# Layer 2 context attention: one place in which an older batch's steps are issued

## The chip, the core and the metric

The kernel runs on one core of a Trainium2 chip. A core has a matrix engine (PE, whose weight loads are shown apart as PEld), a vector engine (DVE), a scalar engine (ACT), a general engine (POOL) and a queue for transfers (SP); each takes its instructions in order, and they wait for each other through semaphores. The metric is device time in microseconds (us) of one execution, the median of several runs. Before the change it is 3500.77 us (three runs, 3495.93 to 3503.63).

## The reference

The reference is a decoder of four layers on x, 8 batches of 256 rows of 256 values; each layer has a self attention, an attention to a context of 77 rows a batch, and a feed-forward part, and each is followed by a layer norm of x plus what the part gave. The change lies in the context attention of layer 2 (`_L2_xattn_ref`) and in the router of the feed-forward part behind it:

```python
q = (x @ q_w.T + q_b).reshape(b, s1, H, hd).transpose(0, 2, 1, 3)
kv = (y @ kv_w.T + kv_b).reshape(b, s2, 2, H, hd).transpose(2, 0, 3, 1, 4)
k, v = (kv[0], kv[1])
q = _layernorm(q, qn_w, qn_b)
k = _layernorm(k, kn_w, kn_b)
q = _apply_rope(q) * scale
attn = jnp.einsum('bhqd,bhkd->bhqk', q, k)
attn = jax.nn.softmax(attn, axis=-1)
o = jnp.einsum('bhqk,bhkd->bhqd', attn, v)
o = o.transpose(0, 2, 1, 3).reshape(b, s1, c)
return o @ out_w.T + out_b
...
# _L2_ffn_ref: 14 routed experts, two of them for each row
gates = jax.nn.softmax(xf @ router_w, axis=-1)
top_v, top_i = jax.lax.top_k(gates, TOP_K)
```

There are 16 heads of 16 values; x has 2048 rows in all, of which each goes to two of the 14 routed experts.

## The kernel before

One program runs the twelve parts one after the other. x stays on chip as 16 tiles of 128 rows, and, transposed, as four tiles `xt`. `l2_xattn` works batch by batch (two tiles of 128 rows). The order of the work is written out by hand, and the build lays it down engine by engine in nearly that order. A pass of the loop for batch b issues:

- `weights(b, q2)`: products of keys and shifted queries (L1837) in two groups, and their exponentials on ACT (L1842);
- `queries(b + 2)`: values and queries (L156 on `cT`, `xt` and `qb`), the query's norm on DVE (L1665 to L1671, L1783);
- `shift(b + 1, ...)`: transposes of the padded queries (L302), the score products (L1814, 32 small matmuls), their maxima on DVE (L1818, eight reductions), then `between`, then the turn of the maxima: eight transposes (L1825) and two additions onto the transposed queries (L1826). With the maximum in an extra row of the query the next pass gets shifted scores;
- as `between`: `weigh(b, e, v)`, products of exponentials and values in two halves (L1856), each copied out (L1862 on ACT, L1858 on DVE);
- `rotated(b + 2, ...)`: the rotary embedding on POOL and DVE (L1794 to L1800).

What ends a batch is put on a list, `todo`, by `self.later`, as a generator. `tick` (line 94) issues the next step of the first entry; a finished entry is taken off and the next one starts in the same tick. `settle_local` (line 110) ticks until no entry that was marked local is left. For each batch the list holds two entries one after the other:

- `heads_out` (line 1391), with `project` and `put_both`: transposes of oT and the division by the row sums (L1398 to L1407); transposes of o (L302); the out projection (L156, `w,oT`) with the residual (L276 on POOL, L281), and the layer norm (L253, L255, POOL L183 and L184, L264); transposes of x into `xt` (L236);
- `Routing.batch` (line 2546): squares of x on ACT (L2554), their root on POOL (`rr`), x scaled (`rx`, L2560), the router products (L156, `rw,xt`), softmax and the two largest (L2578 to L2597), the running counts (L2600, `rbefore`); an empty step; then the rank products (L156, `rsel,upper` and `rbefore,onesb`), ranks and targets (L2609 to L2622), and four scatters of x rows to the experts' slots by POOL (L1041).

In a pass there are ticks in `weights` (two), in `shift` (one before and one behind the score products), in `weigh` (one after each half) and one at the end. Before the change this brings, for the batch before the one that is weighed: o transposes and out projection in `weights`, x transposes and router products in `shift`, the empty step and the rank products in `weigh`; and oT transposes of the batch just weighed at the pass's end. `self.routed` keeps the DVE copy of the second half of weigh behind the running counts.

Behind the stage the feed-forward part starts with `l2_shared` (L1893, L1897, L1907), whose weights `l2s` are loaded on SP and scaled by ACT (L1927), and `tables`, which needs the ranks of all batches.

Of the kernel before, what the change touches and what calls it, by code (L numbers as in the profile page):

```python
# [61 lines left out]
class Build:  # L62
# [1660 lines left out]
    def l2_xattn(self, route):  # L1723
        nc, a = self.nc, self.a
        with ExitStack() as ctx:
# [38 lines left out]
            def queries(b):  # L1764

                v = vps[b % 3]
                ps = self.ps()
                self.mm(ps[:SC, :D], [(self.cT[:, k, b * SC : (b + 1) * SC], W[:, k, 512:768]) for k in range(2)])
                nc.vector.tensor_tensor(
                    v[:SC, :, :16],  # L1770
                    ps[:SC, :D].rearrange("p (h d) -> p h d", h=H),
                    self.row("l2x_kvb")[:SC, D:].rearrange("p (h d) -> p h d", h=H),
                    ALU.add,
                )
                ps = self.ps()
                for t in range(2):
                    self.mm(
                        ps[:, t * D : (t + 1) * D],
                        [(self.xt(k, 2 * b + t), W[:, k, :256]) for k in range(2)] + [(one[:1], qb[:1])],
                    )  # L1780
                r = self.deviations(w2, ps.rearrange("p (n d) -> p n d", d=16), 32)
                q = self.t(w2, [P, 2, H, 16], "q")
                nc.vector.tensor_tensor(  # L1783
                    q.rearrange("p t h d -> p (t h) d"), ps.rearrange("p (n d) -> p n d", d=16),
                    r.unsqueeze(2).to_broadcast([P, 32, 16]), ALU.mult,
                )
                return q, v

            def rotated(b, q, v):
                qp = qpad[b % 3][:, :, :, :16]  # L1790
                over = lambda t: t.unsqueeze(2).to_broadcast([P, 2, H] + list(t.shape[2:]))
                u1, u2 = (self.t(w2, [P, 512], n).rearrange("p (t h d) -> p t h d", t=2, h=H) for n in ("sq", "u2"))
                for u in range(2):
                    nc.gpsimd.tensor_tensor(  # L1794
                        u2[:, :, :, u::2], q[:, :, :, 1 - u :: 2], over(other[:, :, :, u]), ALU.mult
                    )
                flat = lambda t: t.rearrange("p t d u -> p t (d u)")
                nc.vector.tensor_tensor(u1, q, over(flat(own)), ALU.mult)
                nc.vector.tensor_tensor(u1, u1, over(flat(more)), ALU.add)
                nc.gpsimd.tensor_tensor(qp, u1, u2, ALU.add)  # L1800
                return qpad[b % 3], v

            def shift(b, qp, between=None):

                qT = self.t(w2, [P, 4, S], "qT")
                for t in range(2):
                    self.transpose_to(qT[:, :, t * P : (t + 1) * P], qp[:, t].rearrange("p h d -> p (h d)"), 4)
                self.tick()
                tiles = [slice(t * P, (t + 1) * P) for t in range(2)]
                for t, c in enumerate(tiles):  # L1810
                    ps = [self.ps()[:, : 4 * SC].rearrange("p (g s) -> p g s", g=4) for j in range(4)]
                    for g in range(4):
                        for j, r in enumerate(rows):
                            nc.tensor.matmul(  # L1814
                                ps[j][:, g, :], qT[r, g, c], kT[r, g, b * SC : (b + 1) * SC], start=True, stop=True
                            )
                    for j in range(4):
                        nc.vector.tensor_reduce(mxps[t][:, :, j, 16], ps[j], AX.X, ALU.max, negate=True)  # L1818
                self.tick()
                if between is not None:  # L1820
                    between()
                for t, c in enumerate(tiles):
                    pt = self.ps().rearrange("p (g s) -> p g s", g=4)
                    for g in range(4):
                        nc.tensor.transpose(pt[:, g, :], mxps[t][:, g].rearrange("p j d -> p (j d)"), self.ident)  # L1825
                    nc.vector.tensor_tensor(qT[:, :, c], pt, qT[:, :, c], ALU.add)  # L1826
                return qT

            def weights(b, q2):

                e = []
                for gp in range(2):
                    ps = [self.ps()[:SC].rearrange("p (g s) -> p g s", g=2) for j in range(4)]
                    for i in range(2):
                        for j, r in enumerate(rows):
                            g = 2 * gp + i
                            nc.tensor.matmul(  # L1837
                                ps[j][:, i, :], kT[r, g, b * SC : (b + 1) * SC], q2[r, g, :], start=True, stop=True
                            )
                    o = self.t(w2, [SC, 4, 2, S], "e", bufs=2)  # L1840
                    for j in range(4):
                        nc.scalar.activation(o[:, j], ps[j], AF.Exp, scale=0.25)  # L1842
                    e.append(o)
                    self.tick()
                return e

            def weigh(b, e, v):

                o = self.t(w2, [P, 4, S], "oT")
                routed, self.routed = self.routed, None  # L1850
                for gp in range(2):
                    ps = self.ps().rearrange("p (g s) -> p g s", g=2)
                    for i in range(2):
                        for j, r in enumerate(rows):
                            h = 4 * (2 * gp + i) + j
                            nc.tensor.matmul(ps[r, i, :], v[:SC, h, :], e[gp][:, j, i, :], start=True, stop=True)  # L1856
                    if gp:
                        ins = nc.vector.tensor_copy(o[:, 2 * gp : 2 * gp + 2, :], ps)  # L1858
                        if routed is not None:
                            self.after(ins.ins, [routed.ins])  # L1860
                    else:
                        nc.scalar.copy(o[:, 2 * gp : 2 * gp + 2, :], ps)  # L1862
                    self.tick()
                self.settle_local()
                self.later(self.heads_out(b, o, W[:, :, 768:1024], "l2x_ob", w2, route=route))

            self.routed = None
            ahead = [rotated(0, *queries(0))]
            begun = queries(1)
            q2 = shift(0, ahead[0][0])  # L1870
            ahead.append(rotated(1, *begun))
            for b in range(NB):
                e, v = weights(b, q2), ahead[0][1]
                ahead.pop(0)
                if b + 2 < NB:
                    begun = queries(b + 2)
                if b + 1 < NB:
                    q2 = shift(b + 1, ahead[0][0], lambda: weigh(b, e, v))
                else:
                    weigh(b, e, v)  # L1880
                if b + 2 < NB:
                    ahead.append(rotated(b + 2, *begun))
                self.tick()
# [1079 lines left out]
```

## Time and profile before

| | |
|---|---|
| median of the runs | 3500.77 us |
| the profiled execution's own time | 3466.69 us |
| its span, first to last instruction | 3465.0 us |
| mean granted PE clock | 0.913 |
| the stage: first score products to first L1893 | 2436.1 to 2652.8 us |
| starts of the eight score products | 2436.1, 2453.8, 2475.7, 2503.5, 2531.1, 2558.5, 2585.8, 2612.2 us |

The profile is of one execution. Lines of it name start and length in us, the engine, the line of the kernel, the operation, and tiles as out<-in; in square brackets stands how long the engine was idle before it, and what released it. In a table of stretches each engine has its busy time and the number of its instructions. The granted clock is the share of full speed that PE was allowed. A busy PE is not PE at its peak, since matmuls overlap.

### The profile page before, as it was taken

Reading aid. Unit: us, or ns where it says so; the run is one execution under the profiler, and the core shown is the slowest. Engines: PE = TensorE matmul, PEld = TensorE weight load, DVE = VectorE, ACT = ScalarE, POOL = GpSimd, SP = SyncE. Lnnn points to the kernel's source line nnn. Section 1 sums busy time; section 2 is a strip of 40 time slices with the busy share of each in tenths; the row PEclk is TensorE's granted clock in tenths of the full one; section 3 lists DMA queues with packets and bytes.
Section 4 is the critical chain, followed back from the end, with each engine's and each line's share of the span. In section 5 each row is a group of like instructions: output and inputs, shape, how many; then the busy total and the mean of one; then the engine's idle time right before and its main releaser. Section 6 shows DMA issues by size and latency. Waiting matters only on the chain. (4 is left out here: it accounts for less than half of the span.)

```text
span 3465.0 us, 49405 instructions
## 1 busy us (share of the span) xinstructions
PE 3068.0 (89%) x19135; PEld 2169.0 (63%) x19146; DVE 1819.0 (52%) x4852; ACT 1055.4 (30%) x2386; POOL 911.1 (26%) x1370
## 2 busy tenths in 40 slices
PE   4777679989998998998999999898888998888789
PEld 3444357768886666665566776565555886676556
DVE  7887556641005656785111221576675344777652
ACT  4666422222222233332111111343222112344211
POOL 2222323343313211232000000322343454322241
PEclk6777779989999999999999999999777999988899
DMA  9900110025532000001010333100002562000000
GB/s 334 333 1 6 34 42 16 16 94 185 187 128 89 17 28 14 17 17 59 14 37 25 113 131 118 37 20 8 7 19 84 200 210 77 25 1 7 13 6 19
DMA packets 132672, 241.58 MB, mean 70 GB/s; under 512 B 14600, under 2 KB 103952, under 8 KB 124752
## 3 DMA queue, kind: packets, MB, share of 16 engines
q1 hardware_dynamic: 108176, 138.34, 11.8%
q0 software_dynamic: 23104, 98.95, 8.3%
q8 instruction: 155, 2.54, 0.3%
q10 hardware_dynamic: 1152, 1.05, 0.1%
q14 instruction: 85, 0.70, 0.1%
HBM read 158.61 MB, written 79.69 MB: 69 GB/s over the span
## 5 line engine op out<-in xcount | busy, mean ns | idle before, releaser
L156 PE MATMUL ps<-xt,w 128*128 128x256 f32 (+1 forms) x1408 | 444.6, 465 | 8.3 <-issue 8.3
L156 PE MATMUL ps<-w,hT 128*128 128x256 f32 (+1 forms) x1792 | 397.4, 380 | 0.0
L156 PEld LDWEIGHTS ps<-w,hT 128*128 128x128 f32 (+1 forms) x1792 | 330.5, 187 | 55.9 <-issue 6.0
L156 PE MATMUL ps<-gT,w 128*128 128x256 f32 (+1 forms) x1472 | 356.9, 401 | 5.7 <-ACT gT L144 3.0
L156 PEld LDWEIGHTS ps<-xt,w 128*128 128x128 f32 x1408 | 263.8, 194 | 150.5 <-issue 129.8
L156 PEld LDWEIGHTS ps<-gT,w 128*128 128x128 f32 x1472 | 276.8, 191 | 76.1 <-ACT gT L144 3.9
L156 PE MATMUL ps<-w,oT 128*128 128x256 f32 x768 | 184.1, 394 | 12.3 <-DVE oT L1423 11.2
L156 PEld LDWEIGHTS ps<-w,oT 128*128 128x128 f32 x768 | 147.7, 196 | 48.6 <-issue 12.6
L1147 ACT ACTIVATE hT<-ps,more 128x256 f32<-128x256 f32 x152 | 71.9, 473 | 199.1 <-PE ps L156 199.1
L236 PE MATMUL ps<-ident,x 128*128 128x128 f32 x320 | 64.8, 314 | 74.2 <-DVE x L264 57.3
L276 POOL TENSOR_TENSOR xb<-x,rows 128x256 f32<-128x256 f32 x96 | 74.0, 778 | 212.7 <-DVE res L281 205.5
L264 DVE TENSOR_SCALAR x<-res,mv,rs 128x256 f32<-128x256 f32 x128 | 58.8, 459 | 123.0 <-POOL rs L184 123.0
L1158 DVE COPY y<-ps 128x512 f32<-128x512 f32 x41 | 28.3, 690 | 174.6 <-PE ps L156 174.6
L1224 DVE TENSOR_TENSOR hT<-hT,ps 128x512 f32<-128x512 f32 x56 | 38.5, 687 | 150.6 <-PE ps L156 150.6
L686 ACT ACTIVATE e<-ps,nm 128x128 bf16<-128x128 f32 (+1 forms) x256 | 103.7, 459 | 40.1 <-DVE nm L681 24.1
L1220 ACT ACTIVATE hT<-ps 128x512 f32<-128x512 f32 x56 | 33.4, 597 | 238.5 <-PE ps L156 238.5
L1717 POOL TENSOR_TENSOR kpad<-kpad,rows 128x256 f32<-128x256 f32 (+1 forms) x10 | 7.3, 729 | 363.5 <-DVE hu L1666 276.2
L236 PEld LDWEIGHTS ps<-ident,x 128*128 128x128 f32 x320 | 39.5, 155 | 98.9 <-DVE x L264 44.9
L903 POOL TENSOR_TENSOR P<-P,z 128x1232 f32<-128x1232 f32 (+1 forms) x32 | 55.2, 1734 | 167.3 <-DVE z L902 167.3
L970 PE MATMUL ps<-PT,V 77*64 77x256 f32 x512 | 90.8, 413 | 6.9 <-ACT PT L144 4.4
L1581 ACT ACTIVATE f<-ps,neg 128x512 f32<-128x512 f32 x128 | 77.3, 688 | 57.7 <-PE ps L1578 57.7
L1582 DVE SCALAR_TENSOR_TENSOR f<-ps,f 128x512 f32<-128x512 f32 x128 | 79.1, 682 | 26.1 <-ACT f L1581 26.1
(665 smaller groups left out, 6344.7 us busy)
## 6 DMA issues: line engine op xcount, KB each, us to landing
l2x<-zero SPq DMA_DIRECT2D x28, 1024.0 KB, 11.4
l0x<-zero SPq DMA_DIRECT2D x16, 1024.0 KB, 11.4
w<-in_L_ffn_rg SPq DMA_DIRECT2D x8, 1024.0 KB, 7.1
w<-in_L_ffn_ru SPq DMA_DIRECT2D x8, 1024.0 KB, 5.0
w<-in_L_ffn_rd SPq DMA_DIRECT2D x8, 1024.0 KB, 5.4
l2e<-y SPq DMA_DIRECT2D x22, 256.0 KB, 2.3
rows<-in_rows SPq DMA_DIRECT2D x9, 544.0 KB, 3.7
l0e<-y SPq DMA_DIRECT2D x19, 256.0 KB, 2.7
```

Of the source, the lines that this page charges most:

```text
L156: self.nc.tensor.matmul(out, lhsT, rhs, start=(i == 0), stop=(i == last))
L236: self.nc.tensor.transpose(ps[:, k * P : (k + 1) * P], x[:, k * P : (k + 1) * P], self.ident)
L264: nc.vector.tensor_scalar(t, r, mv[:, 0:1], rs, ALU.subtract, ALU.mult)
L276: self.nc.gpsimd.tensor_tensor(t, self.X[i], row, ALU.add)
L686: nc.scalar.activation(e[:, : (t + 1) * P], ps[j][:, i, :], AF.Exp, bias=nm[:, t, h : h + 1], accum_out=z[:, t, h : h + 1],)
L903: eng.tensor_tensor(pr, pr, z.unsqueeze(2).to_broadcast([P, n, SC]), ALU.mult)
L970: nc.tensor.matmul(po[64 * m : 64 * m + 64, :S], V[:, h * 64 : (h + 1) * 64], ahead[n % 2][:, m, :], start=True, stop=True,)
L1147: nc.scalar.activation(hT[:, f + m, :], ps[:, m * 256 : (m + 1) * 256], func, bias=more[:, f + m : f + m + 1])
L1220: nc.scalar.activation(hT[:, f, :], ps, func, **({"bias": bias(f)} if bias else {}))
L1224: nc.vector.tensor_tensor(hT[:, f, :], hT[:, f, :], ps, ALU.mult)
L1581: nc.scalar.activation(f[:, j], ps[j], AF.Exp, bias=neg1)
L1582: self.mark = nc.vector.scalar_tensor_tensor(f[:, j], ps[j], 1.0, f[:, j], ALU.max, ALU.min)
```

## The change

The second half of `weigh` is no longer followed by a tick, and what followed the two halves, `settle_local` and the putting of `heads_out` on the list, becomes a function `end` of its own. It is called when `shift` is done, that is behind the turn of the maxima. In the last pass, without a shift, it is called right after `weigh`.

```diff
                     else:
                         nc.scalar.copy(o[:, 2 * gp : 2 * gp + 2, :], ps)
-                    self.tick()
+                    if not gp:
+                        self.tick()
+                return b, o
+
+            def end(b, o):
                 self.settle_local()
                 self.later(self.heads_out(b, o, W[:, :, 768:1024], "l2x_ob", w2, route=route))
...
+                out = []
                 if b + 1 < NB:
-                    q2 = shift(b + 1, ahead[0][0], lambda: weigh(b, e, v))
+                    q2 = shift(b + 1, ahead[0][0], lambda: out.append(weigh(b, e, v)))
                 else:
-                    weigh(b, e, v)
+                    out.append(weigh(b, e, v))
+                end(*out[0])
                 if b + 2 < NB:
                     ahead.append(rotated(b + 2, *begun))
                 self.tick()
```

With one tick fewer in a pass, and nothing else asking for a step, the remaining ticks find earlier steps of the list than before. No instruction is added or taken away.

## The prediction

> **What bounds the kernel now.** I read the page first, then the one stage that the change touches. The page:
>
> ```profile
> span 3465.0 us, 49405 instructions
> PE 3068.0 (89%) x19135; PEld 2169.0 (63%) x19146; DVE 1819.0 (52%) x4852; ACT 1055.4 (30%) x2386; POOL 911.1 (26%) x1370
> PEclk6777779989999999999999999999777999988899
> ```
>
> PE bounds the kernel as a whole. The context attention of layer 2 lies at 2436 to 2653 us: its three slices of about 87 us are the dip to 7 in the PEclk row. Next, the stretches of the stage. A batch is counted from one start of the score products (L1814) to the next; the columns are the stretch, its length, busy time of PE, PEld, DVE, ACT and POOL, granted clock, DMA share, GB/s:
>
> ```profile
> 2503.50:2531.13 27.63, 23.88 (x196) 17.18 (x196) 18.96 (x70) 7.20 (x19) 11.17 (x16) 0.75 0.06 21
> 2558.50:2585.84 27.34, 22.30 (x196) 15.76 (x196) 19.46 (x70) 7.20 (x19) 11.17 (x16) 0.81 0.06 21
> 2612.23:2652.87 40.64, 30.60 (x245) 21.96 (x245) 22.93 (x95) 11.48 (x28) 13.99 (x23) 0.67 0.34 118
> ...
> 2492.45:2506.10 13.65, 12.45 (x110) 8.65 (x106) 6.69 (x21) 6.50 (x16) 7.07 (x12) 1.00 0.11 38
> 2506.10:2519.75 13.65, 11.10 (x88) 8.38 (x87) 12.16 (x50) 0.71 (x2) 3.59 (x4) 0.50 0.01 2
> ```
>
> A batch takes 27.3 to 27.9 us, no engine fills it, and the clock is two-valued inside it: half speed from the score products to the turn, full speed for the rest. So this stage is a chain between PE and DVE. The waits of PE over five such batches, and the steps of one of them:
>
> ```profile
> PE ps L156 <- DVE rsel L2597: 11.0, 5, 2.7
> PE ps L1814 <- DVE mxp L1818: 5.7, 5, 1.2
> ```
>
> ```profile
> 2503.50 1.13 PE L1814 MATMUL ps<-l2kT,qT 32*128 32x77 f32 x32 [0.16 <-ACT qT L144]
> ...
> 2509.38 1.89 PE L156 MATMUL ps<-rw,xt 128*128 128x14 f32 x8
> ...
> 2511.19 3.64 PE L1856 MATMUL ps<-e,vp 77*32 77x256 f32 x32
> ...
> 2516.29 0.20 PE L156 MATMUL ps<-rsel,upper 128*128 128x14 bf16 x1 [1.46 <-DVE rsel L2597]
> ...
> 2516.71 1.74 PE L1825 MATMUL ps<-ident,mxp 128*128 128x128 f32 x7
> ...
> 2518.24 1.78 PE L1398 MATMUL ps<-ident,oT 128*128 128x128 f32 x8
> ...
> 2523.48 1.99 PE L156 MATMUL ps<-w,oT 128*128 128x256 f32 x8
> ...
> 2525.86 0.17 DVE L255 BATCH_NORM_AGGREGATE mv<-st 128x2 f32<-128x6 f32 x1
> ...
> 2527.71 0.41 DVE L264 TENSOR_SCALAR x<-res,mv,rs 128x256 f32<-128x256 f32 x1 [0.92 <-POOL rs L184]
> ...
> 2529.16 0.41 DVE L264 TENSOR_SCALAR x<-res,mv,rs 128x256 f32<-128x256 f32 x1 [0.95 <-POOL rs L184]
> ```
>
> PE waits 11.0/5 = 2.2 us a batch in front of the rank products (L156, rsel) for the router's selection, with the turn (L1825) behind them though its maxima are ready. That wait is what the change goes at. But the older batch's norm (res, aggregate, x, then rx at 2531.22) runs beside the query products of 2525.10 to 2529.44, where PE has work that does not need it.
>
> **The change, part by part.** *Rank products behind the turn.* The turn's transposes (1.74 us) and its two adds on DVE no longer stand behind the rank products. In a batch where nothing else moves this saves at most the wait and the turn that stood behind it: 1.46 + 1.74 = 3.2 us.
>
> *One step fewer per batch.* The steps of the older batch come off one list, one per tick, and the rank step has an empty step ahead of it. With the second tick of `weigh` gone, the built order lets the rank products and then w,oT fall back in the third batch of the stage (they start at 2436.09, 2453.80, 2475.65 and so on) and the rest in the fourth; from the fifth (now 2531.13), every step of the older batch stands one place later. PE then has: score products, out projection (w,oT), half of weigh, x transposes, other half, turn, router products, half of the weights' products (L1837), rank products, other half, transposes of oT, queries. DVE has the norm, rx, the oT copy and the two adds of the turn behind the eight maxima, then the router's softmax.
>
> I walk one such batch at full clock, from the first score product at 0. The maxima end at 2511.41 - 2503.50 = 7.9 now; without the xt copy (0.33) and two rx (0.62) ahead of them, with an oT copy (0.33), 7.3. Two res and two stats (0.34, 0.34, 0.40, 0.40 to the next) and the aggregate: 9.0. From the aggregate to the first x is 1.85 us (2525.86 to 2527.71), to the second 1.45 more, to rx 2.06 more: 10.8, 12.3, 14.3. PE has done w,oT and half of weigh by about 8.3 and waits about 3 us for x. Two rx 0.62, oT copy 0.60, two adds 1.29: the turn is complete at 16.8, against 2519.17 - 2503.50 = 15.7 now. The router's softmax follows on DVE: 2.7 us without other work between (2638.75 to 2641.43 in the last batch), so rsel at 19.5 and the rank products done at 20.0, against 13.2 now. Half of L1837 1.0 (2519.95 to 2520.98), oT transposes 0.9 (as the eight of qpad, 2529.44 to 2530.37), queries 4.3 (2525.10 to 2529.44), transposes of qpad and o 1.3: next score products at 27.5. So at full clock the batch is no shorter than the 27.4 of now: **0**. The wait for rsel is back (about 2 us: 1.0 us of products stands before it where 3.64 of weigh stood), and a wait for x is new.
>
> *The clock on that path.* Now the half-speed stretch ends 3.46 us after the rank products (2516.29 to 2519.75), in the unbroken PE work that follows them. In the new order unbroken work begins only at 20.0, so the half speed should last till 23.5. At half speed the other half of weigh, the turn and the router products (1.82, 1.74 and 1.89 by their rows) put the softmax back from 16.8 to about 18.5: +1.7. The half of L1837 and the oT transposes take 1.8 each in place of 1.0 and 0.9 (half of weigh takes 1.07 at 2631.42 at full speed, 1.82 above; the oT transposes' 1.78 is above): +1.7. Sum **+3.4** a batch, two full batches: **+6.8**. Bounds 0 (full clock) and +5.1 (two query products of 0.86 at half speed too).
>
> *Third and fourth batch*: the wait ahead of the turn is saved, but the softmax now shares DVE with the turn and half speed lasts past the rank products. Bounds -3.2 and 0 each; I take **0**, by the clock row.
>
> *The seventh batch* (2585.84 to 2612.23, 26.39 us, no queries): 27.5 - 4.3 + 1.7 = 24.9, so -1.5; its softmax may come later by the same 1.7: between -1.5 and +0.2. I take **-0.5**.
>
> *The end.* The before already shows the new order once: in the last batch w,oT starts at 2629.49, weigh's halves (1.07 and 1.54) lie between, and router products come only at 2636.82. In the changed kernel batch 6 is a step further back, weigh runs ahead of its w,oT and covers nothing: 2.6 (1.07 + 1.54) to 3.64 (a whole weigh at half speed); **+3.0**.
>
> *Queues.* SP: the five loads of l2s and l3wd pass ahead of the reload of rows; its first reader is at 2890, so 0, covered by 230 us of L2 FFN; were it not, one landing of 3.7 us. POOL: the same adds, rsqrts and four scatters a batch, the rope product (L1800, 1.27) now between rs and rr; POOL is busy 11.2 of 27.6, the scatters' reader comes after the stage. ACT: two l2s scalings (1.33) now stand between the squares of batch 6: 0 to 1.3, **+0.5**.
>
> The sum: 0 + 6.8 - 0.5 + 3.0 + 0.5 = **+9.8 us**. The profiled execution took 3466.69 (span 3465.0 and 1.69 around it), so 3476.5 on its terms; the median of the runs is 3500.77, 34 us (1.0%) above it, and I add the difference to that: **3510.6 us**.
>
> A rule weighed. "TensorE: Matmul & The Clock Gate", section "Why this matters for your kernels" of the Trainium skill, says that a kernel keeps full speed without PE gaps of over about 3 us. Here the clock fell to 0.50 at 2506.10 with no PE wait above 1.2 us in front of the score products, and no longer one within 10 us before, so the trace does not agree; by the page the new wait of 3 us would just pass, the clock would not fall, and the sum would be that of the first rival.
>
> **The rivals.** *The clock recovers early (other side).* If weigh and turn, now adjacent, bring full speed before the rank products, both middle batches keep 3.2 and the full ones cost 0: -6.4 + 0 - 1.5 + 3.0 + 0.5 = -4.4, 3496.4 us. It decides if PE's stretch between score products and rank products is granted 1.00. For it: full speed came back 3.5 us into unbroken work. Against it: the new wait for x breaks that work.
>
> *The wait is simply gone (faster).* If POOL's rs comes some 3 us sooner and x is there when half of weigh ends, only the saved waits count: -11.0, 3489.8 us. Against it: 1.85 and 1.45 us from aggregate to x in every batch.
>
> *Half speed reaches the queries:* 2 x 5.1 + 3.64 + 1.3 = +15.1, 3515.9 us.
>
> **How the numbers follow.** A change below 0.2% (7 us) can hardly be told from none. Chances: the forecast 0.55 (own range 3505 to 3515; 0.07 of it below +7), half speed further 0.12, clock recovers 0.18, wait gone 0.15. Slower: 0.48 + 0.12 = 0.60; same: 0.07 + 0.18 = 0.25; faster: 0.15. The range leaves out most of the fastest case and the top of the slowest, and adds the runs' own 4 us: 3493 to 3520.
>
> **What would show it.** Right: in the after, batches five and six at 30 to 31 us; a PE wait at L236 for x of 2 to 4 us; L156 still waiting for rsel about 2 us; half clock past the rank products; about 3 us more from the last score products to the first router work of the FFN (L1893 here). Wrong if those batches are at or under 27 us, or the clock in the stage rises above 0.8 while L236 does not wait.

## The result, and the profile after

The changed kernel takes 3515.22 us (median of six runs, 3512.55 to 3521.26) beside 3498.35 us for the kernel before (six runs, 3490.62 to 3503.63): a ratio of 1.0049, 95% interval 1.0033 to 1.0065. That is 16.9 us slower, where +9.8 was forecast.

The page of the profile of the changed kernel (its lines for the span, the busy time, and the granted clock in 40 slices):

```profile
span 3511.4 us, 49401 instructions
PE 3087.6 (88%) x19135; PEld 2169.0 (62%) x19146; DVE 1821.1 (52%) x4852; ACT 1057.4 (30%) x2386; POOL 912.0 (26%) x1370
PEclk6777789989999999999999999998776999988899
```

No work was added, yet PE is busy 19.6 us longer than in the profile before, and the dip to 7 in the clock row reaches 6. The page alone decides nothing, since a second profile of the kernel before (the last experiment) has PE busy for 3092.6 us; the stage has to be read by itself. From the first score product to the first product of the feed-forward part (L1893 before, L1899 now), it went from 216.78 to 241.18 us: +24.4. The stage before, then after (columns as in the prediction: stretch, length, busy time and records of PE, PEld, DVE, ACT, POOL, granted clock, DMA share, GB/s):

```profile
2436.09:2652.87 216.78, 176.68 (x1521) 125.56 (x1521) 142.19 (x503) 59.40 (x144) 79.13 (x110) 0.76 0.10 35
```

```profile
2457.17:2698.35 241.18, 188.64 (x1521) 127.93 (x1521) 142.83 (x503) 61.94 (x144) 79.41 (x110) 0.71 0.09 32
```

Behind it, 812.11 and 813.04 us remain. The two profiled executions also differ by 21 us in unchanged code ahead of the stage. That is scatter between executions: the second profile of the kernel before starts its stage at 2459.67 us, where the first had 2436.09.

The stretches of the stage in the changed kernel: batches five, six and seven, and the end:

```profile
2555.07:2587.92 32.85, 26.13 (x197) 17.54 (x197) 19.62 (x72) 7.73 (x19) 11.42 (x15) 0.69 0.05 17
2587.92:2619.70 31.78, 23.70 (x198) 16.26 (x197) 19.72 (x72) 7.79 (x19) 11.38 (x15) 0.73 0.05 18
2619.70:2648.44 28.74, 22.04 (x181) 15.36 (x180) 19.25 (x70) 7.31 (x18) 11.38 (x15) 0.64 0.04 15
2648.44:2698.35 49.91, 36.43 (x257) 24.21 (x257) 26.39 (x105) 13.02 (x34) 16.94 (x29) 0.63 0.29 99
```

A fifth batch that took 27.37 us with 22.28 us of PE now takes 32.85 with 26.13, of the same 197 records, at a clock of 0.69 in place of 0.81. The end holds 12 records more than before (257, it was 245). Over the whole stage PE is busy 188.64 us (176.68 before) and idle 52.54 (40.10): the 24.4 us are 12.0 of the same products done more slowly and 12.4 of waits.

The waits of PE over the third to seventh batch (line, what it waited for, us in total, times, longest), in the kernel before those for the norm's x alone, then in the changed kernel:

```profile
PE ps L236 <- DVE mv L255: 1.9, 1, 1.9
PE ps L236 <- DVE x L264: 1.0, 1, 1.0
```

```profile
PE ps L236 <- DVE mv L255: 8.8, 3, 4.0
PE ps L1814 <- DVE mxp L1818: 8.3, 5, 3.6
PE ps L156 <- DVE rsel L2603: 7.5, 5, 3.5
PE ps L236 <- DVE x L264: 6.7, 3, 2.3
```

The wait for the router's selection fell from 11.0 to 7.5 us, and 15.5 us of waiting for the norm's x (L236) are there where 2.9 were. The steps of the sixth batch, in order of time (start, length, engine, line, operation, tiles; idle time and its releaser in brackets):

```profile
2591.65 1.99 PE L156 MATMUL ps<-w,oT 128*128 128x256 f32 x8
...
2593.57 1.07 PE L1856 MATMUL ps<-e,vp 77*32 77x256 f32 x16
...
2598.65 0.66 PE L236 MATMUL ps<-ident,x 128*128 128x128 f32 x2 [4.01 <-DVE mv L255]
...
2601.37 0.66 PE L236 MATMUL ps<-ident,x 128*128 128x128 f32 x2 [2.07 <-DVE x L264]
...
2601.96 1.94 PE L1856 MATMUL ps<-e,vp 77*32 77x256 f32 x16
...
2603.83 1.97 PE L1825 MATMUL ps<-ident,mxp 128*128 128x128 f32 x8
...
2610.09 0.19 PE L156 MATMUL ps<-rsel,upper 128*128 128x14 bf16 x1 [0.84 <-DVE rsel L2603]
...
2612.32 1.94 PE L1398 MATMUL ps<-ident,oT 128*128 128x128 f32 x8
```

It is the order that the prediction walked. The out projection stands behind the score products, half of `weigh` (1.07 us, full clock) covers little of the norm, PE waits 4.0 and 2.1 us for x, and the other half takes 1.94 us: the clock has fallen to 0.50 meanwhile (from 2597.0 to 2614.1 by the clock's record, 17.1 us; 10.2 in the fifth and sixth batch before).

Batch by batch, against the kernel before:

| | before | after | difference | forecast |
|---|---|---|---|---|
| batches 1 and 2 | 39.6 | 38.1 | -1.5 | 0 |
| batch 3 | 27.85 | 30.97 | +3.1 | 0 |
| batch 4 | 27.64 | 28.86 | +1.2 | 0 |
| batch 5 | 27.37 | 32.85 | +5.5 | +3.4 |
| batch 6 | 27.35 | 31.78 | +4.4 | +3.4 |
| batch 7 | 26.39 | 28.75 | +2.4 | -0.5 |
| the end | 40.64 | 49.91 | +9.3 | +3.5 |

The -1.5 of the first two batches is not the change's: the second profile of the kernel before takes 38.05 us for them.

### The profile page after: what moved, and what is told of

The parts are those of the page before. It is cut to its first block, busy times and chain, and to the rows that moved or that the text cites. A ratio compares the mean times of both kernels' runs of the same rounds, so it can differ in the third digit from the quotient of the medians.

```text
span 3511.4 us, 49401 instructions
## 1 busy us (share of the span) xinstructions
PE 3087.6 (88%) x19135; PEld 2169.0 (62%) x19146; DVE 1821.1 (52%) x4852; ACT 1057.4 (30%) x2386; POOL 912.0 (26%) x1370
## 3 DMA queue, kind: packets, MB, share of 16 engines
q1 hardware_dynamic: 108176, 138.34, 11.8%
q10 hardware_dynamic: 1152, 1.05, 0.1%
## 5 line engine op out<-in xcount | busy, mean ns | idle before, releaser
L236 PE MATMUL ps<-ident,x 128*128 128x128 f32 x320 | 66.3, 317 | 95.0 <-DVE x L264 70.8
L264 DVE TENSOR_SCALAR x<-res,mv,rs 128x256 f32<-128x256 f32 x128 | 61.5, 480 | 123.6 <-POOL rs L184 123.6
L1158 DVE COPY y<-ps 128x512 f32<-128x512 f32 x41 | 28.3, 691 | 171.5 <-PE ps L156 165.6
L236 PEld LDWEIGHTS ps<-ident,x 128*128 128x128 f32 x320 | 39.2, 156 | 123.9 <-issue 61.4
L1582 DVE SCALAR_TENSOR_TENSOR f<-ps,f 128x512 f32<-128x512 f32 x128 | 79.1, 682 | 26.2 <-ACT f L1581 26.2
```

The source lines that it names most:

```text
L236: self.nc.tensor.transpose(ps[:, k * P : (k + 1) * P], x[:, k * P : (k + 1) * P], self.ident)
L264: nc.vector.tensor_scalar(t, r, mv[:, 0:1], rs, ALU.subtract, ALU.mult)
L1582: self.mark = nc.vector.scalar_tensor_tensor(f[:, j], ps[j], 1.0, f[:, j], ALU.max, ALU.min)
```

## The experiments

The change does two things at once: it puts the rank products behind the turn, and it takes a step out of each pass, which puts the older batch's steps a place later. Theory: the lost place costs, through waits for x and a longer half-speed stretch, and the exchange is free or a gain. Rival: the exchange itself costs.

The time that stands beside a measured one is that of the kernel before in the same comparison; it differs between comparisons (3469.87 to 3498.26 us). Stages, batches and waits are those of one profiled execution each.

**The exchange alone.** One more step inside `end`, so that all other steps stay at their old places:

```diff
             def end(b, o):
+                self.tick()
                 self.settle_local()
```

> The changed kernel, with one more step of the list issued inside `end`, ahead of settle_local. Each pass so has as many steps as before the change, and PE's order is the old one but for one exchange: the rank products come behind the turn. Theory (the lost place costs, the exchange does not): w,oT stays in front of the queries, the stage takes 205 to 218 us (216.8 before, 241.2 with the whole change), PE does not wait for x at L236 over 0.5 us, and the time is 0 to 10 us under the kernel before. Rival (the exchange itself costs, because the turn's two adds on DVE and the rank work get in each other's way): the stage takes 225 us or more and the time is 8 us or more above the kernel before.

Measured: 3498.51 us beside 3469.87, ratio 1.0080 (1.0066 to 1.0095), and a stage of 239.43 us. The rival holds: batches three to seven take 33.48, 32.15, 30.80, 30.79 and 31.37 us with every step but one at its old place, and PE waits 17.6 us in them for rsel, where it waited 11.0. One such batch:

```profile
2589.50 0.17 DVE L2586 TENSOR_TENSOR rs<-ps,rm 128x28 f32<-128x28 f32 x1
...
2591.21 1.97 PE L1825 MATMUL ps<-ident,mxp 128*128 128x128 f32 x8
2592.43 0.69 DVE L1826 TENSOR_TENSOR qT<-ps,qT 128x512 f32<-128x512 f32 x1 [2.76 <-PE ps L1825]
...
2593.04 0.17 DVE L2588 TENSOR_REDUCE rm<-rs 128x2 f32<-128x28 f32 x1
...
2596.69 0.17 PE L156 MATMUL ps<-rsel,upper 128*128 128x14 bf16 x1 [3.51 <-DVE rsel L2604]
```

DVE's queue has changed too. The turn's first add (L1826) now stands between the softmax's subtraction (L2586) and its sum (L2588). The exponentials were ready at 2590.4, but DVE stands 2.76 us at the add, which waits for PE's turn, which waits behind `weigh`. So rsel is done 15.5 us after the first score product (2581.17), where in the fifth batch before it was 12.5 (2543.67 - 2531.13), and the rank products wait 3.5 us for it with nothing left to cover it.

**The lost place alone.** The kernel before with the step behind the second half of `weigh` taken away, and `settle_local` and `later` at their old place ahead of the turn:

```diff
-                    self.tick()
+                    if not gp:
+                        self.tick()
```

> The kernel before with only the step behind the second half of weigh taken away; settle_local and the putting on the list stay inside weigh, ahead of the turn. In this order the router products come ahead of the turn and the rank products behind it. Theory (the lost place costs): batches five and six take 30 to 33 us, PE waits 4 to 6 us a batch for x at L236, the stage takes 232 to 245 us, the time is 10 to 20 us above the kernel before. Rival (the exchange costs, not the place): batches at 27 to 28 us and the time within 5 us of the kernel before.

Measured: 3487.68 beside 3469.87 us, ratio 1.0059 (1.0039 to 1.0079), stage 237.69 us; batches five and six 33.16 and 33.63, with 14.8 + 11.8 us of waits for x in the stage. As the theory expected, with batches even longer than its 30 to 33 us. The lost place is not wholly alone here: the rank products come behind the turn in this order too, and the third batch (30.99 us, with a wait of 3.5 us for rsel) is that of the changed kernel. In batches five to seven PE does not wait for rsel at all, so their length is put down to the lost place. Either half of the change makes the stage some 20 us longer by itself, and the two do not add up: once the router's products come behind the turn, the turn's adds have nothing left to push back (the same dependency in the changed kernel, below).

**DVE's order restored.** The kernel of the first experiment, with the turn's adds held behind the router's running counts, as they stood before:

```diff
+                self.chosen = routed
...
-                    nc.vector.tensor_tensor(qT[:, :, c], pt, qT[:, :, c], ALU.add)
+                    ins = nc.vector.tensor_tensor(qT[:, :, c], pt, qT[:, :, c], ALU.add)
+                    if between is not None and self.chosen is not None:
+                        self.after(ins.ins, [self.chosen.ins])
```

> The kernel with the rank products behind the turn and all steps at their old places (e1_order), with the two adds of the turn on DVE held behind the router's running counts by a dependency, as DVE's order was before the change. Theory (the exchange costs because the turn's adds slip ahead of the softmax's sum on DVE, which then stands 2.8 us waiting for PE's turn): rsel comes 12.5 to 13 us after the first score product in place of 15.3, PE waits about 1 us or less for it, a steady batch takes 26 to 27.5 us in place of 30.8 to 33.5, the stage 205 to 217, and the time is 0 to 10 us under the kernel before. Rival (the half clock or the place of the rank products costs, whatever DVE does): batches at 29 us or more, time 10 us or more above the kernel before.

Measured: 3491.01 us beside 3497.78, ratio 0.9976 (0.9963 to 0.9989): faster than the kernel before. The stage takes 214.42 us. Its steps in one batch, and the stretch they lie in:

```profile
2561.40 3.64 PE L1859 MATMUL ps<-e,vp 77*32 77x256 f32 x32
...
2564.97 1.97 PE L1825 MATMUL ps<-ident,mxp 128*128 128x128 f32 x8
...
2566.26 0.19 DVE L2607 TENSOR_TENSOR rsel<-rhot 128x28 bf16<-128x28 f32 x1
...
2566.74 0.22 PE L156 MATMUL ps<-rsel,upper 128*128 128x14 bf16 x1
...
2567.94 1.28 DVE L1826 TENSOR_TENSOR qT<-ps,qT 128x512 f32<-128x512 f32 x2
```

```profile
2553.71:2580.96 27.25, 23.28 (x196) 16.25 (x197) 18.90 (x70) 7.20 (x19) 11.11 (x16) 0.81 0.06 20
```

rsel is done 12.7 us after the first score product (2553.71), PE works through the turn in the time in which it used to wait, and the wait for rsel is gone. One dependency on DVE turns +28 us into -7, each against the kernel before in its own comparison, and a stage of 239.43 us into 214.42: the cause of the exchange's cost is settled. Only with that order is the exchange a gain, and a small one: 0.1 to 0.5 us a batch against the first trace of the kernel before, 0.8 to 1.2 against the second, where the prediction had it save up to 3.2.

**The same dependency in the changed kernel** (the diff is the one above, on the changed kernel):

> The changed kernel with the dependency of e6_dve: the two adds of the turn stand behind the running counts of the router, where those were issued before. In batches three and four the router is still ahead of the turn, from the fifth on its products come behind it. Theory (two causes, each with its batches): batches three and four go from 30.97 and 28.86 us to 27 to 28, the fifth and later stay within 0.7 us of what they were, the stage goes from 241.2 to 234 to 238 us, the time stays 10 us or more above the kernel before. Rival (one cause, DVE's order): all batches come back to 27 to 28 and the stage to under 225 us.

Measured: 3516.61 beside 3498.26 us, ratio 1.0056 (1.0037 to 1.0075), stage 237.78. The third batch falls to 27.56 us, the fourth, against the theory, stays at 28.85, and the later ones don't move (32.87, 31.81, 28.76, end 49.86). So DVE's order cost 3.4 us in the changed kernel, in the third batch alone. There the changed kernel's own trace had it: DVE is idle for 3.78 us at the first add, with the softmax's sum behind it:

```profile
2503.78 0.17 DVE L2585 TENSOR_TENSOR rs<-ps,rm 128x28 f32<-128x28 f32 x1
...
2507.74 0.69 DVE L1826 TENSOR_TENSOR qT<-ps,qT 128x512 f32<-128x512 f32 x1 [3.78 <-PE ps L1825]
2508.35 0.17 DVE L2587 TENSOR_REDUCE rm<-rs 128x2 f32<-128x28 f32 x1
```

**What the wait for x is worth.** The norm's scale without POOL's reciprocal root, in this stage alone; once on the changed kernel, once on the kernel before:

```diff
-        nc.vector.tensor_scalar(t, r, mv[:, 0:1], rs, ALU.subtract, ALU.mult)
+        nc.vector.tensor_scalar(t, r, mv[:, 0:1], mv[:, 1:2] if self.short else rs, ALU.subtract, ALU.mult)
```

> The changed kernel; in the context attention of layer 2 alone, x is scaled by the variance itself instead of by POOL's reciprocal root, which is still worked out but which nothing waits for (the norm of that part is so left out; later values differ, so the stage alone is read). Theory (in the changed order the batch is set by the older batch's norm, because PE waits 4 to 6 us for x): the waits at L236 fall to 1 to 3 us a batch, the fifth and sixth batch from 32.9 and 31.8 us to 28 to 30, and the stage from 241 to 222 to 232 us. Rival (the router's softmax and the half clock set it, the wait for x only moves): the batches stay at 31 us or more and the stage at 236 or more.

> The kernel before with the same edit as e5_norsq: in the context attention of layer 2 x is scaled by the variance, and nothing waits for POOL's reciprocal root. Theory (the norm is covered by the queries in the old order and by nothing in the new one): the steady batches stay within 0.5 us of 27.4 us, only the last stretch gets shorter, and the stage falls by 3 to 10 us, from 216.8 to 207 to 214, where the changed kernel's fell by 22.2. Rival (the norm weighs the same in both orders, and e5 only took it out): the stage falls by 15 us or more.

Measured: the changed kernel's stage falls from 241.18 to 219.02 us (batches five and six 30.08 and 28.73, with waits of 3.1 us each ahead of the x transposes in place of 4.7 and 6.1), that of the kernel before to 202.24. The stages of the two, the changed kernel first:

```profile
2454.70:2673.72 219.02, 180.24 (x1522) 123.25 (x1521) 139.31 (x503) 61.88 (x144) 78.55 (x108) 0.74 0.10 35
```

```profile
2457.35:2659.59 202.24, 168.35 (x1522) 118.57 (x1521) 141.34 (x503) 61.47 (x144) 78.06 (x107) 0.78 0.11 37
```

By the first alone the theory would have looked proved: 22.2 us of the 24.4 come back. The second takes most of that away. The same edit is worth 14.5 us in the old order too, more than the 3 to 10 expected and just under the rival's 15, half of it in the end (40.64 to 33.33 us). Against the second trace of the kernel before, which is of the same comparison and whose stage is 218.62 us, it is worth 16.4 us: the rival's figure. What the change costs without the root is 219.02 - 202.24 = 16.8 us, so the wait for the root accounts for 24.4 - 16.8 = 7.6 us of the difference by the first trace of the kernel before, and for 22.6 - 16.8 = 5.8 by the second. And of the 16.8, 11.9 (180.24 - 168.35) is PE's busy time: as much as with the root (12.0 by the first trace, 10.3 by the second). The slower products are a second part of the cost, which does not go away with the wait.

**The clock.** Ten products that nobody reads, ahead of the x transposes, where PE waits:

```diff
                     if not gp:
+                        pf = self.ps()
+                        for n in range(10):
+                            nc.tensor.matmul(pf[:, :D], self.ident, W[:, 0, :D], start=True, stop=True)
                         self.tick()
```

> The changed kernel, with ten products of 128x128 by 128x256 of which nobody reads the result, in each pass between the first half of weigh and the x transposes, where PE waits 4 to 6 us for x. They take 2.5 us at full clock and 5 at half, 8 passes. Theory (half of the loss is the clock: PE busy grew by 12.0 of the stage's 24.4 us with the same products): the granted clock of the stage rises from 0.71 to 0.78 or more, batches five and six go from 32.9 and 31.8 to 28 to 30 us, and the time falls to within 8 us of the kernel before in spite of the added products. Rival (DVE and POOL set the batch, whatever the clock): batches five and six stay at 31 to 33 us or grow, and the time is 14 us or more above the kernel before.

Measured: 3492.02 beside 3469.87 us, ratio 1.0069 (1.0053 to 1.0085); stage 236.91 us at a clock of 0.84. The sixth batch:

```profile
2575.42:2606.06 30.64, 26.71 (x218) 19.57 (x217) 19.37 (x72) 7.67 (x19) 11.41 (x15) 0.83 0.05 18
```

The ten take 4.58 us at full clock, not 2.5: the trace has two records for such a product, and the estimate counted records. Without them PE is busy 26.71 - 4.58 = 22.1 us in the batch, where the changed kernel needs 23.70 and the kernel before 22.30. Half speed takes 10.2 us of this batch, by the clock's record, where it took 17.1. So the changed kernel's longer PE time is the clock, as the theory has it, and with the clock back the batch is 1.1 us shorter in spite of 4.58 us of added work. The size was missed: the batch was to take 28 to 30 us and the time to come within 8 us of the kernel before, and it is 22 us above, as the rival had it. The added products cost more than the clock gives.

**The same in the kernel before.** Six such products where it waits for rsel:

```diff
                             self.after(ins.ins, [routed.ins])
+                        pf = self.ps()
+                        for n in range(6):
+                            nc.tensor.matmul(pf[:, :D], self.ident, W[:, 0, :D], start=True, stop=True)
```

> The kernel before, with six products of 128x128 by 128x256 that nobody reads between the second half of weigh and the rank products, where PE waits 1.5 to 2.7 us for rsel. By the ten of e4_filler (4.58 us at full clock) they take 2.7 us at full clock and 5.4 at half. Theory (the half clock lasts because PE's columns are few there): the half-speed stretch ends 3 to 7 us sooner in a batch, turn and oT transposes fall from 1.7 to 1.0 us each, the granted clock of the stage goes from 0.76 to 0.85 or more; with up to 2.7 us of added products sticking out the batch stays within 1.5 us of 27.4 and the time within 10 us of the kernel before. Rival (the clock doesn't follow the products): the clock stays below 0.8, batches take 29 to 31 us and the time is 10 us or more above.

Measured: 3517.21 beside 3497.78 us, ratio 1.0058 (1.0039 to 1.0077); stage 240.52 us, clock 0.79, batches 30.6 to 30.8 us. PE in one of them:

```profile
2569.77 4.64 PE L1863 MATMUL ps<-w,ident 128*128 128x256 f32 x12
...
2574.50 0.96 PE L1825 MATMUL ps<-ident,mxp 128*128 128x128 f32 x7
2575.29 1.12 PE L1398 MATMUL ps<-ident,oT 128*128 128x128 f32 x8
```

The turn's seven transposes take 0.96 us (1.74 before) and the oT transposes 1.12 (1.72), as the theory has it. But this does not show that the products brought the clock back. The half-speed stretch of this batch lasts 10.2 us, as in the fifth batch before, and ends 14.6 us after the first score product in place of 16.0, where 3 to 7 us sooner was expected; the turn now starts at 15.5, where it started at 12.7. So it is at full clock mostly because it comes later. The six take 4.64 us, most of it at half clock, in place of a wait of 2.7 at most, and clock, batches and time are all the rival's.

**The end.** The changed kernel with the missing step put back in the last pass:

```diff
-                    if not gp:
+                    if not gp or b + 1 == NB:
                         self.tick()
```

> The changed kernel, with the step behind the second half of weigh kept in the last pass alone. Theory (the +9.3 us from the last score products to the first work of the feed-forward part come of weigh being issued ahead of batch 6's steps): that stretch goes from 49.9 to 42 to 46 us, and the time is 3 to 8 us under the changed kernel, so 8 to 14 above the kernel before. Rival (batch 6 is late by then whatever the last pass issues): 48 to 51 us and the time of the changed kernel, 14 to 20 above.

Measured: 3493.74 beside 3469.87 us, ratio 1.0082 (1.0062 to 1.0102); the end 49.86 us, the length that the rival expected. But it settles nothing: in the built order PE's steps of the last pass stay where they were, so the step put back moved nothing that PE does there. What the end holds is read from the counts above instead: 12 records more, which are the eight of an out projection and the four of a batch's x transposes. No run tests it.

**Both kernels again.**

> The changed kernel as it is, on the chip of this comparison. Theory (the whole difference lies in the stage, which was 24.4 us longer in the two traces): ratio 1.006 to 1.008, stage 239 to 243 us, batches as in the first trace. Rival (the difference depends on more than the stage): ratio 1.0033 to 1.0055 with a stage of 241 again, so that some 7 us come back elsewhere.

> The kernel before as it is, for a trace on the chip of this comparison. Theory (the stage has the same length on every chip and in every run, and the scatter of the medians lies outside it): stage 216.5 to 217.0 us, batches as in the first trace, whatever the total. Rival (the stage scatters with the total): another stage by over 1 us.

Measured: the changed kernel again at ratio 1.0054 (1.0035 to 1.0072; medians 3520.80 and 3497.78), with a stage of 241.18 us as in its first trace; the kernel before with a stage of 218.62 where the first trace had 216.78:

```profile
2459.67:2678.29 218.62, 178.31 (x1521) 126.37 (x1521) 139.74 (x503) 60.97 (x144) 78.73 (x109) 0.76 0.10 35
```

The first expectation can't be decided by the ratio, whose interval holds both. (The ratios are taken as recorded; the quotient of the two medians here is 1.0066.) The second fell: the old order has at least two courses, one with batches of 27.4 us and one with 28.2 (the clock in the fifth is 0.81 or 0.76). So the change costs 22.6 to 24.4 us in the stage. Against this second trace the rows of the table are 0.0, +2.8, +0.7, +4.4, +3.6, +1.4 and +9.6 us.

The medians differ by 16.9 us in the first comparison and by 23.0 here. Why the first is less than the stage's difference is left open; its interval reaches 22.7 us. The changed kernel's two profiled executions differ by 14.6 us (3511.39 and 3525.98 us of span with the same stage), of which 13.7 lie behind the stage (813.04 and 826.78 us).

## Why the prediction was right, and where it was wrong

The sign, the wait that goes, the wait for x that takes its place and the longer half-speed stretch are all there. The sum of +9.8 is short of the stage's +22.6 to +24.4. That the measured 3515.22 us lies in the stated 3493 to 3520 is in part luck: the stage's difference, put on the 3498.35 us of the kernel before, gives 3521 to 3523. The signs named for being right came, but larger than stated: batches five and six at 32.9 and 31.8 us for 30 to 31, waits for x of 4.7 and 6.1 us for 2 to 4, an end longer by 9.3 us for about 3.

- *Batches three and four, 0 each.* This step failed. It said that the wait ahead of the turn is saved and its bounds were -3.2 and 0: a loss was left out without a reason. The third batch lost 3.1 us, and the dependency of one experiment gave 3.4 back. The prediction walked PE's new order and took DVE's order as given by data; the trace shows DVE standing 3.78 us at the turn's add with the softmax behind it. The same cause makes the exchange alone cost 3.4 to 5.6 us a batch, where the prediction's first part had it save up to 3.2. The fourth batch's +1.2 has another cause. In its trace PE stands 3.64 us ahead of the second group of score products, where it stood 1.09, for maxima of which the first starts 4.7 us after the first score product in place of 3.4; the older batch's norm (L281 to L264) stands ahead of it on DVE. This is read from the trace, and no run tests it.
- *Batches five and six, +3.4 each.* Right mechanism, undersized: +5.5 and +4.4. The walk had first x at 10.8, second x at 12.3, the turn complete at 18.5 in its half-clock case, which makes rsel 21.2; the sixth batch has 10.2, 12.0, 18.6 and 22.1. The fifth has nearly the same four. So both run as walked up to the turn. PE's waits for x, 4.7 and 6.1 us where about 3 was walked, are longer because the second x took 1.34 us in both, where the row of before had 0.41, and in the sixth because PE has half of `weigh` done at 6.7 us, where the walk had 8.3. The term that was too small lies behind the turn: the softmax starts only when the router products, 1.73 us at half clock, are done, at 19.4, where the walk let it start with the turn's end at 18.5. That 0.9 is most of what the sixth batch is over the forecast. The fifth is 1.1 us longer still: half speed lasts to 28.3 us of the batch (26.2 in the sixth; 23.5 was walked) and so into the first of the query products (1.91 us for `w,cT`, 1.05 at full clock), which is what the third rival described.
- *The wait for rsel.* About 2 us were walked with half of L1837 at 1.0; at half clock that half takes 2.00 and the wait is 0.84. The two misses cancel.
- *Batch seven, -0.5.* Measured +2.4 (+1.4 by the second trace): the walk took its clock for nearly that of before; it was 0.64, where it was 0.80.
- *The end, +3.0 and +0.5.* Measured +9.3, the largest miss. The step costed only the cover that `weigh` no longer gives. It left out that with the steps a place later, one more out projection and a batch's x transposes (12 records) come behind the last score products, with their own waits, and that all of it runs at a mean clock of 0.63: +5.8 us busy and +3.4 idle. This is read from the trace; the run made to test it moved nothing.
- *The rivals.* The clock did not recover early (0.69 and 0.73 in the full batches). "The wait is simply gone" was given a condition, that x comes some 3 us sooner. The runs without the root come nearer to it without meeting it, since PE still waits 3.1 us in each of batches five and six, and the change still costs 16.8 us there. That speaks against this rival and does not refute it. "Half speed reaches the queries" was seen in the fifth batch; its +15.1 is nearest to the measured 16.9, but by a sum that also lacks the third batch and most of the end.
- *The rule weighed.* "TensorE: Matmul & The Clock Gate" of the Trainium skill, section "Why this matters for your kernels", asks for no PE gap over about 3 us. In the changed kernel's fifth batch the longest gaps are 2.41 and 2.32 us and half speed lasts 17.1 us; in the fastest variant no gap of a middle batch is over 1.2 us and half speed still takes 10.2 of 27.25. The measurement disagrees with the rule in both. In the changed kernel's sixth batch the gap is 4.01 us and the clock does fall within it, so that batch does not speak against the rule.

Put together, not as exact shares, since the parts overlap: of the 22.6 to 24.4 us some 5.8 to 7.6 are PE waiting for the norm's root, 3.4 are DVE's order in the third batch, and 10.3 to 12.0 are the same products at a lower clock (of which 1.9 go with DVE's order).

## What to carry to other kernels

When a step is moved on one engine, look at what the build does on the others: a short add slipped ahead of a softmax on DVE cost more than the wait that the move took away, and one dependency made the same move a gain. A step that is removed from a list of steps delays everything behind it and leaves its work in the end of the stage, where nothing covers it; count the records there. And an edit that brings the time back shows a cause only if the same edit does not do the same to the kernel before.

## What the runs showed of the hardware that was not expected

The runs speak for a clock that goes by how much PE does rather than by gaps alone: in every variant it fell to half in every batch from the third on, with waits of 1.2 us and of 4.0 us alike, and ten products put into the wait for x cut half speed in batches five and six from 17.1 us at a stretch to 10.2. The half-speed stretches came in steps of about 3.4 us (10.2, 13.7, 17.1 and 20.5 us, and some shorter and longer ones, in these traces), so a small delay may cost a whole step more at half speed.

Some DVE operations stretch while POOL works on 512 elements: the second x took 1.34 us beside POOL's 1.26 us of L1800 (2599.82 to 2601.08), the first, with no POOL work of that size beside it, 0.41. The trace of before has the same pair: a DVE operation of 28 elements (L2583) takes 1.15 us at 2541.14, beside L1800 at 2540.99, and 0.19 us in the changed kernel's sixth batch. Not all do: the maxima (L1818) beside L1800 at 2439.87 in the trace of before take 0.47 us each, as elsewhere. This was seen in the rows and not tested by a run of its own.
